# A two-layer graph network on one core: the ReLU of an attention head moved from ScalarE to one VectorE product, a residual input made later, and a half-speed TensorE in the planner that writes the order

## Chip, cores and metric

The kernel runs on one core of one Trainium2 chip. The metric is device time in microseconds (us) of one execution; the profile adds, for one execution, what every engine did and when. In what follows PE is TensorE (its matmuls; PEld its weight loads), DVE is VectorE, ACT is ScalarE, POOL is GpSimd and SP is SyncE.

## The reference

Sixteen graphs of 1024 nodes with 256 features go through two layers, all in float32. Cut to what matters:

```python
# layer 0: graph attention with 4 heads of 64 features, one edge type present
h = einsum('bnd,hde->bhne', x, W)
weight = leaky_relu(e_src[:, None] + e_dst[None, :]);  weight[adj == 0] = -1e9
dst = softmax(weight) @ h + bias
out = relu(dst) + h                       # per head
out = (out - mean) / sqrt(var + 1e-6) * gamma + beta       # per head
x = layernorm(x + out)
# layer 1: self-attention with 8 heads of 32 features, query = key = value, then an MLP
n = layernorm(x);  a = softmax(where(adj > 0, n n^T / sqrt(32), -inf)) @ n
x1 = x + a;  y = layernorm(x1)
x = layernorm(x + x1 + gelu(y @ W1 + b1) @ W2 + b2)
```

## The kernel before

**Tiling.** A graph is cut into 8 blocks of 128 rows and 2 halves of 512 queries. There is no loop on the chip: Python writes out all instructions of the 16 graphs, one list for each engine, and the engines run their lists in that order (the four compute engines are scheduled by hand).

**Two streams.** `layer0()` and `layer1()` are Python generators, and the writer takes steps from one or the other, so that layer 0 of graph b+1 is interleaved with layer 1 of graph b. Layer 0 of a graph is `prepare` (transposes of `xk` and of the adjacency block `ak`, products with `w0e`, into `acc` banks of PSUM) and `attention0` (for each half and head two groups of 64 matmuls `acc<-v,p`, whose weights `p` are products on DVE). Layer 1 is `attention1` (64 steps in two halves, two groups of heads and eight key blocks: four matmuls `ps<-nT`, four exponentials on ACT, two mask products on DVE, then `po<-p,v`, `po<-p,unit`, `po<-v,p`) and `mlp` (`ps<-yT,w_sb`, GELU on ACT into `hid`, `po<-w_sb,hid`).

**Chains.** What follows a head or a half is a generator too, called a chain. `residual0` is the one the change rewrites: when a head of layer 0 is complete in its `acc` bank, with the sums of the weights in a 65th column, it takes the reciprocal of the sums (`ranges<-acc` on DVE), lets ACT write `relu<-acc,ranges` in four pieces of 128x64, and adds the result to `hb` on DVE. `after0` then normalises a pair of heads, and after the last pair makes the whole row's norm: `sq<-hb,t,r` on ACT (the tile `normed`), its transposes `acc<-ident,sq`, the scaled copies `nT`, the transposes back `acc<-ident,nT`, the copies `v` (the tile `v1`), and at its end `x1`, four ACT products of 128x256, which layer 1 needs as its residual input only after its attention. A chain says with `yield engine, needs...` on what it waits; `advance()` runs it when the planner's clock says that these are there. `finish_norms(b, n)` runs a half's chain to its end at once, if layer 1 asks for the half before that.

**Banks.** `bank0` hands out two PSUM banks (`acc0`, `acc1`) in turn. A bank is free when the chain that reads it has been written down; on the chip the first matmul into it waits for the last read.

**The planner.** The class `Pace` wraps every engine. `enter` keeps for each engine the time when it becomes free, for each tile when it is written and read, and adds `cost` for each instruction. These times decide nothing on the chip, they decide the order only: which stream goes next, and when a chain is advanced. `COURSE` says how far layer 0 is to be for each amount of layer 1 done: a list of (work of layer 1, graphs of layer 0), linear between. Because every instruction passes through `Engine.call`, nearly all rows of the profile carry line 61; rows are told apart by their tiles. Names in the profile leave out trailing digits, so `v0` and `v1` both read `v`, `x1` reads `x`, and `p0` reads `p`.

Of the kernel before, what the change touches and what calls it, by code (L numbers as in the profile page):

```python
# [35 lines left out]
AF = mybir.ActivationFunctionType  # L36
OP = mybir.AluOpType
PSUM = bass.MemoryType.PSUM

P = 128  # L40
# [9 lines left out]
class Engine:  # L50


    def __init__(self, pace, name):
        self.pace, self.name = pace, name
# [35 lines left out]
class Pace:  # L90
# [5 lines left out]
    def __init__(self, nc):  # L96
        self.nc = nc
        self.free = dict.fromkeys(self.LATENCY, 0.0)
        self.written, self.read = {}, {}
        self.array = self.table = self.last = None  # L100

        self.born = self.settle = lambda tile: None
        for name in self.LATENCY:
            setattr(self, name, Engine(self, name))
# [38 lines left out]
    def enter(self, engine, op, args, kwargs):  # L143
        aps = [a for a in (*args, *kwargs.values()) if isinstance(a, bass.AP)]
        out, ins = aps[0].tensor.name, [a.tensor.name for a in aps[1:]]
        if op == "dma_start":
            start = max(self.now(), self.through(out))
            self.written[out] = start + self.LATENCY["sync"]
            return
        start = max(  # L150
            [self.free[engine], self.read.get(out, 0.0)] + [self.written.get(i, 0.0) for i in ins if i != out]
        )
        end = self.free[engine] = start + self.cost(engine, op, aps, args[2] if len(args) > 2 else None)
        self.written[out] = max(self.written.get(out, 0.0), end + self.LATENCY[engine])
        if "accum_out" in kwargs:
            out = kwargs["accum_out"].tensor.name
            self.written[out] = max(self.written.get(out, 0.0), end + self.LATENCY[engine])
        for i in ins:
            self.read[i] = max(self.read.get(i, 0.0), end)
# [3 lines left out]
def fast_path(  # L163
# [24 lines left out]
    nc = Pace(tc.nc)  # L188
    B, N, D = x.shape
    H0, _, HO = w0.shape  # L190
# [9 lines left out]
    BPH = HALF // P  # L200
# [66 lines left out]
    for i, (src, queue, _) in enumerate(terms):  # L267
        for pair in range(H0 // PAIR):
# [3 lines left out]
                    tensor=src.tensor,  # L272
# [11 lines left out]
    for i, (_, _, dst) in enumerate(terms):  # L284
        for c in range(DC):
            t = two.tile([P, H0, HO], F32, name="z")
# [17 lines left out]
    def at_time(t):  # L304
        return lambda: t
# [28 lines left out]
    def power(src, n, name):  # L334
        r = small.tile([P, n], F32, name=name)
        nc.gpsimd.tensor_tensor(r, src, mhalf[:, :n], op=OP.pow)
        return r

    def statistics(src, mv):
        st = small.tile([P, 6], F32, name="st", passing=True)  # L340
        nc.vector.bn_stats(st, src)
        nc.vector.bn_aggr(mv, st)

    def minus_mean(mean, r, n):
        t = small.tile([P, n], F32, name=f"t{n}")
        nc.vector.scalar_tensor_tensor(t, mean, -1.0, r, op0=OP.mult, op1=OP.mult)
        return t
# [97 lines left out]
    def complete(chain):  # L445

        for item in list(chains):
            if item[0] is chain:
                while item in chains:
                    run(item)  # L450


    def load_x(t, b, k, count):
        nc.sync.dma_start(t, x[b, k * P : (k + count) * P, :].rearrange("(g p) d -> p g d", p=P))
# [161 lines left out]
    def residual0(av, h, rinv):  # L616

        t = two.tile([P, BPH, HO], F32, name="relu")
        nc.vector.reciprocal(rinv, av[:, :, HO])
        yield "scalar", rinv  # L620
        for q in range(BPH):
            nc.scalar.activation(t[:, q, :], av[:, q, 0:HO], AF.Relu, scale=rinv[:, q : q + 1])
        yield "vector", t
        nc.vector.tensor_add(h, h, t)

    def after0(b, n, hd, o):


        for first in range(hd + 1):
            complete(residuals[b, n, first])  # L630
        rowwise = [P, BPH, D]
        heads = slice((hd - PAIR + 1) * HO, (hd + 1) * HO)
        oh = o[:, :, heads].rearrange("p g (h e) -> p g h e", e=HO)
        per_head = [P, BPH, PAIR, HO]
        s = small.tile([P, BPH, PAIR], F32, name="s0")
        nc.vector.tensor_reduce(s, oh, axis=mybir.AxisListType.X, op=OP.add)
        nc.vector.scalar_tensor_tensor(
            oh, s[:, :, :, None].to_broadcast(per_head), -1.0 / HO, oh, op0=OP.mult, op1=OP.add
        )
        yield "scalar", o  # L640
        sq = two.tile([P, BPH, PAIR * HO], F32, name="oT1")
        nc.scalar.activation(sq, o[:, :, heads], AF.Square)
        if hd == H0 - 1:
            xl = one.tile(rowwise, F32, name="xl")
            load_x(xl, b, n * BPH, BPH)
        yield "vector", sq
        v = small.tile([P, BPH, PAIR], F32, name="v0s")
        nc.vector.tensor_reduce(
            v, sq.rearrange("p g (h e) -> p g h e", e=HO), axis=mybir.AxisListType.X, op=OP.add
        )  # L650
        nc.vector.tensor_scalar(v, v, 1.0 / HO, EPS_HEAD, op0=OP.mult, op1=OP.add)
        r = power(v.rearrange("p g e -> p (g e)"), BPH * PAIR, "r0").rearrange("p (g e) -> p g e", e=PAIR)
        pair = o[:, :, heads]
        nc.vector.tensor_mul(pair, pair, lng0_r[:, None, heads].to_broadcast([P, BPH, PAIR * HO]))
        if hd == H0 - 1:
            nc.vector.tensor_add(xl, xl, lnb0_r[:, None, :].to_broadcast(rowwise))
        yield "vector", r
        nc.vector.tensor_mul(oh, oh, r[:, :, :, None].to_broadcast(per_head))
        if hd < H0 - 1:
            return  # L660
        complete(norms[b, n, PAIR - 1])
        nc.vector.tensor_add(o, o, xl)
        yield "vector", o
        mv = small.tile([P, BPH, 2], F32, name="mv0")
        for g in range(BPH):
            statistics(o[:, g, :], mv[:, g, :])

        v2 = small.tile([P, 2, BPH], F32, name="v2")  # L670
        nc.vector.tensor_scalar(v2[:, 0, :], mv[:, :, 1], 1.0 + EPS, EPS * EPS, op0=OP.mult, op1=OP.add)
        r2 = power(v2[:, 0, :], BPH, "r2")
        nc.vector.tensor_scalar(v2[:, 1, :], mv[:, :, 1], EPS, None, op0=OP.add)
        r3 = power(v2[:, 1, :], BPH, "r3")
        yield "vector", r2
        t = minus_mean(mv[:, :, 0], r2, BPH)
        yield "scalar", t
        normed = one.tile(rowwise, F32, name="sq")
        scale_shift(normed, o, t, r2, BPH)
        yield "tensor", normed, side_ready  # L680
        nT = two.tile([P, DC, HALF], F32, name="nT")
        for g in range(0, BPH, GB):
            transpose_rows(nT[:, :, g * P : (g + GB) * P], normed[:, g : g + GB, :], g1_c, be1_c)
            yield "tensor", normed, side_ready
        yield "tensor", nT, side_ready
        v1 = two.tile([P, BPH, H1, HD + 1], F32, name="v1")
        nc.vector.memset(v1[:, :, :, HD], 1.0)
        for g in range(0, BPH, GB):
            pt = side_bank([P, GB, DC, P])
            for i in range(GB):  # L690
                for c in range(DC):
                    nc.tensor.transpose(pt[:, i, c, :], nT[:, c, (g + i) * P : (g + i + 1) * P], ident)
            nc.scalar.copy(
                v1[:, g : g + GB, :, 0:HD], pt.rearrange("p g c (h e) -> p g (c h) e", e=HD)
            )
            yield "tensor", nT, side_ready
        handed[b, n] = [None, v1, nT]
        yield "vector", r3

        ratio = small.tile([P, BPH], F32, name="ratio")  # L700
        nc.vector.tensor_mul(ratio, v2[:, 0, :], r2)
        nc.vector.tensor_mul(ratio, ratio, r3)
        yield "scalar", ratio
        x1 = three.tile(rowwise, F32, name="x1")
        for g in range(BPH):
            nc.scalar.mul(x1[:, g, :], normed[:, g, :], ratio[:, g : g + 1])
        handed[b, n][0] = x1
# [271 lines left out]
    ATTN1 = 2.0 + 2.5 * (NH * NB * H1 // QUAD)  # L979
    WORK1 = ATTN1 + NB // GB * (1.75 * FC / 2 + 3.5 * GB)  # L980
    SLACK = 0.06
    COURSE = [(0.0, 1.0), (ATTN1, 1.40), (WORK1 - 10.0, 2.0), (WORK1, 2.0)]

    def wanted():
        b, done = place[1]
        for (start, low), (end, high) in zip(COURSE, COURSE[1:]):
            if done < end:
                return b + low + (high - low) * (done - start) / (end - start)
        return b + COURSE[-1][1]

# [470 lines left out]
```

## Time and profile before

| what | value |
| --- | --- |
| median of 3 runs | 3663.35 us (3662.82 to 3672.89) |
| the profiled execution: its own time, its span | 3667.81 us, 3665.6 us |
| mean granted TensorE clock | 0.976 |
| busy share: PE, PEld, DVE, ACT, POOL | 96%, 65%, 77%, 60%, 12% |
| instructions | 142190 |
| `relu<-acc,ranges` on ACT, 128x64 | 512 times, 319 ns each, 118.2 us |
| `hb<-hb,relu` on DVE, 128x256 | 128 times, 424 ns each, 54.2 us |
| `x<-sq,ratio` on ACT (the tile x1), 128x256 | 128 times, 501 ns each, 54.6 us |

A row of groups names line, engine, operation, output and inputs, shapes and count, then the busy time, the mean of one instruction, and the idle time of that engine just before, with what ended it. A row of the timeline gives start, length, engine, output and inputs and a count, and in square brackets the idle time before it. A float32 matmul appears as two records. The row of a window gives the busy time of each engine, and behind POOL the granted TensorE clock, where 1.00 is full speed, the share of the DMA engines and the GB/s moved.

### The profile page before, as it was taken

Reading aid. Unit: us, or ns where it says so; the run is one execution under the profiler, and the core shown is the slowest. Engines: PE = TensorE matmul, PEld = TensorE weight load, DVE = VectorE, ACT = ScalarE, POOL = GpSimd, SP = SyncE. Lnnn points to the kernel's source line nnn. Section 1 sums busy time; section 2 is a strip of 40 time slices with the busy share of each in tenths; the row PEclk is TensorE's granted clock in tenths of the full one; section 3 lists DMA queues with packets and bytes.
Section 4 is the critical chain, followed back from the end, with each engine's and each line's share of the span. In section 5 each row is a group of like instructions: output and inputs, shape, how many; then the busy total and the mean of one; then the engine's idle time right before and its main releaser. Section 6 shows DMA issues by size and latency. Waiting matters only on the chain.

```text
span 3665.6 us, 142190 instructions
## 1 busy us (share of the span) xinstructions
PE 3506.3 (96%) x64673; PEld 2368.4 (65%) x64673; DVE 2840.2 (77%) x4882; ACT 2191.5 (60%) x5024; POOL 428.7 (12%) x424
## 2 busy tenths in 40 slices
PE   6899999999999999999999999999999999999998
PEld 4567575675856658576585766757567585665846
DVE  5787787878878787787887868778787887878784
ACT  2665746557475574746647466574755747557474
POOL 0102011010110101101020110201101011010100
PEclk9899999999999999999999999999999999999999
DMA  4111101011010110201101011110101102010000
GB/s 102 33 18 33 29 14 37 15 37 24 15 41 11 36 23 16 45 6 40 20 27 34 13 35 17 33 29 14 39 14 35 26 14 43 11 36 9 16 6 14
DMA packets 77525, 97.30 MB, mean 27 GB/s; under 512 B 9072, under 2 KB 59760, under 8 KB 76912
## 3 DMA queue, kind: packets, MB, share of 16 engines
q0 software_dynamic: 18432, 33.56, 6.1%
q1 hardware_dynamic: 56896, 53.50, 4.6%
q8 instruction: 508, 8.32, 0.9%
q10 hardware_dynamic: 1584, 1.05, 0.1%
q14 instruction: 105, 0.86, 0.1%
HBM read 104.87 MB, written 16.78 MB: 33 GB/s over the span
## 4 chain that ended last, share of the span: by engine, by line
PE 87%; ACT 8%; DVE 3%; issue 1%; DMA 0%; ACTq 0%; POOL 0%; POOLq 0%; DVEq 0%
PE ps L61 33%; PE po L61 33%; PE acc L61 21%; ACT p L61 3%; DVE p L61 2%; ACT mask L61 1%; ACT sq L61 1%; ACT nT L61 1%; ACT v L61 0%; ACT relu L61 0%; DMA w0e<-in_L_gnn_W_dram 0%; ACT z L61 0%; ACT cb L61 0%; DVE z L61 0%; ACT oT L61 0%
## 5 line engine op out<-in xcount | busy, mean ns | idle before, releaser
L61 ACT ACTIVATE p<-ps 128x512 f32<-128x512 f32 x2048 | 1061.8, 617 | 402.1 <-PE ps L61 402.1
L61 DVE TENSOR_TENSOR p<-p,mask 128x1024 f32<-128x1024 f32 x1024 | 1187.9, 1218 | 103.0 <-ACT p L61 101.3
L61 PE MATMUL ps<-nT 32*128 32x512 f32 x4096 | 795.4, 654 | 11.0 <-ACT cb L61 9.8
L61 DVE SCALAR_TENSOR_TENSOR p<-cb,dinv,mask 128x512 f32<-128x512 f32 x1024 | 698.9, 744 | 28.6 <-ACT cb L61 28.6
L61 PEld LDWEIGHTS po<-v,p 128*32 128x32 f32 x32768 | 401.1, 111 | 323.5 <-issue 279.7
L61 PE MATMUL acc<-v,p 128*64 128x65 f32 x16384 | 546.2, 225 | 28.6 <-ACT relu L61 13.2
L61 PEld LDWEIGHTS acc<-v,p 128*64 128x64 f32 x16384 | 507.4, 139 | 96.1 <-issue 47.4
L61 PE MATMUL po<-p,v 128*32 128x512 f32 x2048 | 559.1, 621 | 0.0
L61 PE MATMUL po<-p,unit 128*32 128x512 f32 x2048 | 558.5, 621 | 0.0
L61 ACT ACTIVATE hid<-ps,b_sb 128x256 f32<-128x256 f32 x512 | 241.4, 476 | 437.1 <-PE ps L61 435.0
L61 PE MATMUL ps<-yT,w_sb 128*128 128x256 f32 x2048 | 480.0, 384 | 0.0
L61 PE MATMUL po<-w_sb,hid 128*128 128x256 f32 x2048 | 477.0, 384 | 0.0
L61 PEld LDWEIGHTS po<-w_sb,hid 128*128 128x128 f32 x2048 | 382.4, 190 | 74.5 <-issue 22.7
L61 PEld LDWEIGHTS ps<-yT,w_sb 128*128 128x128 f32 x2048 | 379.8, 190 | 51.8
L61 PE MATMUL po<-v,p 128*32 128x33 f32 x32768 | 392.5, 199 | 4.6 <-issue 4.5
L61 PEld LDWEIGHTS ps<-nT 32*128 32x128 f32 x4096 | 284.9, 187 | 153.2 <-ACT p L61 52.0
L61 PEld LDWEIGHTS po<-p,v 128*32 128x32 f32 x2048 | 79.4, 109 | 339.9 <-DVE p L61 171.9
L61 POOL TENSOR_TENSOR r<-v,mhalf 128x1 f32<-128x1 f32 (+1 forms) x192 | 168.0, 880 | 574.7 <-DVE v L61 540.1
L61 DVE TENSOR_TENSOR z<-acc,bias_r 128x256 f32<-128x256 f32 x128 | 54.2, 423 | 219.5 <-ACT hb L61 217.8
L61 POOL TENSOR_TENSOR r<-v1s,mhalf 128x4 f32<-128x4 f32 x32 | 61.9, 1934 | 1214.9 <-DVE v1s L61 1214.9
L61 POOL TENSOR_TENSOR r<-v0s,mhalf 128x8 f32<-128x8 f32 x64 | 128.9, 2014 | 522.6 <-DVE v0s L61 522.6
L61 POOL DMA_DIRECT2D ak<-in_adj_dram x128 | 69.8, 545 | 914.3 <-PE acc L61 903.9
(113 smaller groups left out, 3078.8 us busy)
## 6 DMA issues: line engine op xcount, KB each, us to landing
ak<-in_adj_dram POOLq DMA_DIRECT2D x128, 256.0 KB, 4.0
xk<-in_x_dram SPq DMA_DIRECT2D x64, 256.0 KB, 3.4
xl<-in_x_dram SPq DMA_DIRECT2D x32, 512.0 KB, 4.0
out_dram<-z SPq DMA_DIRECT2D x128, 128.0 KB, 1.7
w_sb<-in_L_gnn_W_dram SPq DMA_DIRECT2D x2, 1024.0 KB, 6.6
v<-in_L_gnn_a_src_dram SPq DMA_DIRECT2D x2, 320.0 KB, 4.9
v<-in_L_gnn_a_dst_dram ACTq DMA_DIRECT2D x1, 320.0 KB, 7.0
xl<-in_L_gnn_a_dst_dram ACTq DMA_DIRECT2D x1, 320.0 KB, 6.2
```

Of the source, the lines that this page charges most:

```text
L61: return method(*args, **kwargs)
```

## The change

Four edits. `residual0` no longer goes to ACT: after the reciprocal one DVE instruction takes the maximum with zero and multiplies with the reciprocal, spread over the 64 columns of each piece, and the add to `hb` follows without a `yield`. `after0` asks for a time 12 us later on the planner's clock before it writes `x1`. `Pace.enter` doubles the cost of a TensorE instruction that starts within 3 us after TensorE waited for more than 1.5 us. `COURSE` has 1.42 in place of 1.40 at the end of layer 1's attention.

```diff
@@ class Pace, __init__
+        self.slow = 0.0
@@ class Pace, enter
-        end = self.free[engine] = start + self.cost(engine, op, aps, args[2] if len(args) > 2 else None)
+        cost = self.cost(engine, op, aps, args[2] if len(args) > 2 else None)
+        if engine == "tensor":
+            if start > self.free[engine] + 1.5:
+                self.slow = start + 3.0
+            if start < self.slow:
+                cost *= 2.0
+        end = self.free[engine] = start + cost
@@ residual0
         nc.vector.reciprocal(rinv, av[:, :, HO])
-        yield "scalar", rinv
-        for q in range(BPH):
-            nc.scalar.activation(t[:, q, :], av[:, q, 0:HO], AF.Relu, scale=rinv[:, q : q + 1])
-        yield "vector", t
+        nc.vector.scalar_tensor_tensor(
+            t, av[:, :, 0:HO], 0.0, rinv[:, :, None].to_broadcast([P, BPH, HO]), op0=OP.max, op1=OP.mult
+        )
         nc.vector.tensor_add(h, h, t)
+        yield from ()
@@ after0
-        yield "scalar", ratio
+        yield "scalar", ratio, at_time(nc.now() + 12.0)
         x1 = three.tile(rowwise, F32, name="x1")
@@ fast_path
-    COURSE = [(0.0, 1.0), (ATTN1, 1.40), (WORK1 - 10.0, 2.0), (WORK1, 2.0)]
+    COURSE = [(0.0, 1.0), (ATTN1, 1.42), (WORK1 - 10.0, 2.0), (WORK1, 2.0)]
```

## The prediction

> **What bounds the kernel now.** I read the page's busy line first, then the waits of PE, then stretches of 5 us with their clock, then the timeline where they are bad.
>
> ```profile
> PE 3506.3 (96%) x64673; PEld 2368.4 (65%) x64673; DVE 2840.2 (77%) x4882; ACT 2191.5 (60%) x5024; POOL 428.7 (12%) x424
> ...
> PE 87%; ACT 8%; DVE 3%; issue 1%; DMA 0%; ACTq 0%; POOL 0%; POOLq 0%; DVEq 0%
> ```
>
> PE is busy for 96% and holds 87% of the chain that ended last. Two things can be had: PE's idle time, 3665.6 - 3506.3 = 159 us, and the time at lowered clock, 3665.6 x (1 - 0.976) = 88 us. The waits of PE (total, times, longest) say for whom it is idle:
>
> ```profile
> PE acc L61 <- ACT mask L61: 37.3, 34, 9.7
> PE acc L61 <- ACT nT L61: 18.7, 19, 1.1
> PE acc L61 <- ACT relu L61: 14.5, 17, 1.4
> PE acc L61 <- DVE z L61: 13.1, 37, 1.8
> ...
> PE acc L61 <- ACT v L61: 10.7, 15, 0.7
> ```
>
> The counts of 15 to 19 and 34 say one or two places per graph. A graph takes 223 us (the `sq` at 1700.3 returns at 1923.6), and its worst place is where layer 1 of a graph begins:
>
> ```profile
> 1700.00:1705.00 5.00, 3.84 (x14) 2.08 (x13) 3.23 (x5) 5.00 (x12) 0.00 (x0) 0.63 0.72 128
> 1705.00:1710.00 5.00, 5.00 (x80) 2.18 (x76) 4.06 (x8) 3.65 (x11) 0.00 (x0) 0.50 0.00 0
> 1710.00:1715.00 5.00, 3.16 (x38) 2.29 (x26) 1.58 (x2) 2.98 (x7) 0.00 (x0) 0.85 0.01 3
> ```
>
> Here ACT is full in the first row, PE idles in the first and third, and the clock is 0.63, 0.50 and 0.85. The timeline names the waits (brackets), and a second place later in the graph:
>
> ```profile
> 1700.83 1.72 PE L61 MATMUL acc<-w0e,xT 128*128 128x264 f32 x4 [0.28 <-DVE z L61]
> ...
> 1703.43 1.11 PE L61 MATMUL acc<-ident,sq 128*128 128x128 f32 x4 [0.88 <-ACT mask L61]
> ...
> 1712.35 1.09 PE L61 MATMUL acc<-ident,nT 128*128 128x128 f32 x8 [1.11 <-ACT nT L61]
> ...
> 1714.17 0.66 PE L61 MATMUL acc<-ident,xk 128*128 128x128 f32 x4 [0.73 <-ACT v L61]
> ...
> 1813.38 0.95 ACT L61 ACTIVATE relu<-acc,ranges 128x64 f32<-128x64 f32 x4
> 1814.36 0.42 DVE L61 TENSOR_TENSOR hb<-hb,relu 128x256 f32<-128x256 f32 x1 [1.67 <-ACT relu L61]
> 1814.38 2.08 PE L61 MATMUL acc<-v,p 128*64 128x65 f32 x64 [0.79 <-ACT relu L61]
> ```
>
> The boundary costs 0.28 + 0.88 + 1.11 + 0.73 = 3.0 us of idle per graph, and the clock. The relu costs 0.79 us: the bank is free only when ACT has read it, and ACT came to it after four exponentials.
>
> [...] with the run cut into 4 us slices the 14 boundaries from 356 to 3268 us lose (slice times one minus clock, summed) close to 1.7, 3.4, 5.1 or 6.8 us, half of one to four such windows; 63 us in all, 4.5 each. [...] 128x256 takes 425 ns in `o<-acc,ranges` from PSUM and 424 in `hb<-hb,relu` from SBUF. [...]
>
> **Part 1, the relu.** Gone from ACT: 512 x 319 ns = 118.2 us. New on DVE: 128 products of 128x256 with a spread operand out of PSUM; no row shows this form, the nearest is `o<-acc,ranges` (425 ns, spread operand, PSUM)[...]; I take 0.43, 128 x 0.43 = 55 us (bounds 54 to 64). DVE also loses a wait: before `hb<-hb,relu` it stood idle for 156.4 us in 94 cases, mask products queued behind. So DVE ends about 100 us freer, though busier on paper (79%). The bank is now released in DVE's own queue, ahead of the weights `p` for the next group that would use the bank, so PE cannot wait for the relu longer than for its own weights. The 14.5 us go. What is late next there is DVE's mask product: at 1824.18 PE waits 0.41 in the middle of `po<-v,p` (4.5 us in 9 such cases). DVE is full from 1814 to 1826 and now gets 1.67 - 0.43 = 1.2 us back; but the changed order leaves no `acc` group between the last steps of layer 1's attention as a filler, so I book 2 of the 4.5. In the first 110 us layer 0 runs alone and DVE is the bound there: eight products add 3.4 us, the waits for relu that vanish give 2.36 + 0.20 + 0.43; nil. **Sum: -16.5 us.**
>
> **Part 2, the order.** I compared the compiled lists of both kernels. The same matmuls run, changes between matmul shapes are 2098 against 2099, and SP and POOL have equally many rows (DMA issues and powers), so nothing is added. From graph 1 to 13 all graphs have one pattern, so one boundary counts for 15. In it the second transpose of `sq` goes ahead of the first `po` group, a full step (`ps<-nT`, then `po`) lies between the transposes of `nT` and those of `xk`, and ACT writes `sq` ahead of `z` and the small copies. By the durations of the trace: exponentials end at 1699.38; `sq` takes 1.96, to 1701.34; `z` and copies 0.94, to 1702.28; DVE's `z` 0.42 more, so the second `w0e` product begins at 1702.77 in place of 1700.83: **1.94 us more wait**. `mask` ends at 1703.38 as before, so the 0.88 go, and `sq` is transposed at 1704.5, 1.06 later. Then `ps` and the second `sq` to 1709.3; `nT` on ACT to 1710.7; the `po` group covers it until 1712.05 at half clock: 1.11 gone. The `v` copies end near 1713.8, and a step of 2.7 us covers them: 0.73 gone. Per graph 1.94 - 0.88 - 1.11 - 0.73 = -0.78; 15 times, **-11.8 us**. Bounds: +1.06 if the later waits come back elsewhere, -2.7 if `z` is on time.
>
> The clock: from 1704.5 PE now has no gap until the `xk` transposes[...]. That ends the cases of four windows (five of 14) a window or more earlier; against it stands a single gap of 2.2 us. I take half a window less on average, 0.5 x 1.7 x 15 = **-12.8 us** (bounds: one window more, +25; two less, -50).
>
> The steps moved take their DMAs along: the second `ak` turn of the boundary comes one step (3 us) later, and with it POOL's load of the block three ahead; POOL idles 18.8 us before that issue and the load lands in 4.0, so nothing waits.
>
> **Part 3, x1 later.** 128 x 501 ns stay on ACT. For a graph's second half nothing moves: layer 1 asks for it, the chain is forced to its end, and `x1` follows the copies `v` directly in both lists. It delays the next exponentials by 1.7 us, against which PE has a `po` group (1.6). In the first half it lies in the MLP stage, where PE shows 5.00 of 5.00 from 1830 to 1910: nil.
>
> **Total:** -16.5 - 11.8 - 12.8 = -41 us. The profiled execution took 3667.8, so about 3627 for one like it; it stands 4.5 above the median 3663.35, so 3622 against the median.
>
> **Rivals.**
> - *The single gap halves the clock for longer (slower).* [...] With one window more, 1.7, and +1.06 of gaps: 15 x 2.77 = +41.5, less 16.5: +25, **3688**. It decides once the clock costs more than 1.1 us more per graph with the later gaps back. For it: one to four windows happen now[...]. Against: PE is gapless afterwards.
> - *Nothing but the relu.* Boundary gains and losses cancel, or new waits on DVE (55 us more work) eat them: -5 to -16, **3653**. For it: ACT is full at the boundary before and after.
> - *The half clock nearly goes.* If `z` arrives early and one window remains, clock 4.5 - 1.7 = 2.8 and idle 2.0 less per graph: 15 x 4.8 + 16.5 = -88, **3575**.
> - *The planner's edits do nothing*: excluded, since the lists differ.
>
> **How the numbers follow.** Forecast 0.60, slower rival 0.13, relu only 0.12, clock gone 0.15. A difference of 0.3% (11 us) is about what a measurement can tell from none. Faster: 0.60 + 0.15 and a part of relu only = 0.77; same 0.10; slower 0.13. The range takes in most of the third rival and stops short of the slower one: 3565 to 3662.
>
> **What would show it.** Right: no wait of PE for relu; PE's waits for `nT` and `v` near zero; one wait for `z` of about 2 us per graph; the mean clock at 0.979 or more; ACT busy near 2073, DVE near 2895; `relu` on DVE at 0.43 us. Wrong: a clock under 0.976, a `z` wait well under 1 us, or new waits of PE for DVE's `p`.

## The result, and the profile after

The changed kernel takes 3603.46 us (median of 4 runs, 3601.67 to 3610.08) against 3663.09 us (4 runs): 59.6 us less, ratio 0.9835 with the 95% interval 0.9813 to 0.9856. The forecast was 3622, range 3565 to 3662: right in sign and in range, and a third short in size (41 of 60). The profiled execution has a span of 3608.3 us, 57.3 below that of before, at a mean clock of 0.981.

The page's busy line and the engines' shares of the chain, after:

```profile
PE 3478.7 (96%) x64673; PEld 2365.7 (66%) x64673; DVE 2901.0 (80%) x5010; ACT 2088.0 (58%) x4512; POOL 419.1 (12%) x424
...
PE 91%; ACT 6%; DVE 2%; issue 1%; DMA 0%; ACTq 0%; POOL 0%; POOLq 0%; DVEq 0%
```

PE still bounds the kernel. Its idle time fell from 159.3 to 129.6 us, its busy time by 27.6 us for the same matmuls. The waits of PE (total, times, longest):

```profile
PE acc L61 <- DVE z L61: 41.4, 22, 6.0
PE acc L61 <- ACT mask L61: 18.8, 19, 10.3
...
PE acc L61 <- ACT nT L61: 3.2, 7, 1.1
...
PE acc L61 <- DVE relu L61: 2.0, 1, 2.0
...
PE acc L61 <- ACT v L61: 0.7, 1, 0.7
```

The 14.5 us for ACT's relu are gone (one wait of 2.0 for DVE's, at 114 us, is left), `nT` fell by 15.5, `v` by 10.0, `mask` by 18.5, and `z` rose by 28.3. The same boundary as before, in 5 us stretches, with the one wait of PE that the timeline shows between 1676 and 1692 us, and the new product by its tile (minimum, median, maximum in ns; first and last start in us):

```profile
1675.00:1680.00 5.00, 2.78 (x10) 1.46 (x9) 2.22 (x4) 5.00 (x14) 0.58 (x2) 0.79 0.70 131
1680.00:1685.00 5.00, 5.00 (x23) 2.59 (x21) 4.61 (x6) 4.00 (x12) 0.00 (x0) 0.53 0.00 0
1685.00:1690.00 5.00, 4.97 (x122) 2.54 (x123) 2.92 (x6) 4.84 (x11) 0.00 (x0) 1.00 0.01 3
```

```profile
1679.21 2.13 PE L61 MATMUL acc<-w0e,xT 128*128 128x264 f32 x4 [2.22 <-DVE z L61]
```

```profile
L61 DVE SCALAR_TENSOR_TENSOR relu<-acc,ranges x128: 423/425/426, 62.1 to 3414.6; 128x256 f32<-128x256 f32 x128
```

The wait is the one that the prediction worked out, 0.28 + 1.94 = 2.22 us. After it the timeline shows no further wait of PE, and the clock is full again in the third stretch. From the `sq` of graph 1 (356.04 us before, 357.99 after) to that of graph 14 (3266.02 and 3212.77) a graph takes 223.84 and 219.60 us, so these 13 graphs hold 55.2 of the 57.3 us.

To see the clock I cut the stretch from 12 us ahead of each boundary's `sq` to 24 us behind it into slices of 1 us; twice the sum of one minus clock is the time at half clock. A window, below, is 3.41 us at half clock: in the traces of before and changed the stretches at 0.50 between 300 and 3400 us last 3.41 us, or two (before: up to four) times that. Means over the 13 boundaries of graphs 2 to 14, of one profiled execution each; the rows from relu_swap on are the experiments told below:

| kernel | ratio to before, 95% | half clock per boundary, us | PE idle there, us |
| --- | --- | --- | --- |
| before | 1 | 8.9 | 3.4 |
| changed | 0.9835 (0.9813 to 0.9856) | 4.7 | 2.3 |
| relu_swap | 0.9944 (0.9926 to 0.9961) | 8.9 | 3.5 |
| plan_only | 0.9912 (0.9894 to 0.9930) | 5.8 | 1.7 |
| relu_only | 1.0022 (1.0013 to 1.0031) | 4.5 | 3.8 |
| no_slow | 0.9987 (0.9978 to 0.9996) | 5.3 | 3.8 |
| no_course | 0.9842 (0.9827 to 0.9857) | 4.5 | 2.3 |
| sq_late | 0.9885 (0.9866 to 0.9904) | 5.3 | 1.7 |
| warm | 0.9793 (0.9779 to 0.9806) | 0.0 | 0.7 |
| warm2 | 0.9799 (0.9782 to 0.9815) | 0.0 | 1.5 |
| warm_sq | 0.9795 (0.9782 to 0.9808) | 1.3 | 1.0 |
| warm_before | 0.9906 (0.9890 to 0.9923) | 2.6 | 2.6 |

### The profile page after: what moved, and what is told of

Read it like the earlier page. It is cut to its first block, busy times and chain, and to the rows that moved or that the text cites. A ratio compares the mean times of both kernels' runs of the same rounds, so it can differ in the third digit from the quotient of the medians.

```text
span 3608.3 us, 141736 instructions
## 1 busy us (share of the span) xinstructions
PE 3478.7 (96%) x64673; PEld 2365.7 (66%) x64673; DVE 2901.0 (80%) x5010; ACT 2088.0 (58%) x4512; POOL 419.1 (12%) x424
## 4 chain that ended last, share of the span: by engine, by line
PE 91%; ACT 6%; DVE 2%; issue 1%; DMA 0%; ACTq 0%; POOL 0%; POOLq 0%; DVEq 0%
PE po L61 35%; PE ps L61 34%; PE acc L61 22%; ACT p L61 2%; ACT mask L61 1%; DVE p L61 1%; ACT sq L61 1%; ACT xT L61 0%; ACT z L61 0%; ACT nT L61 0%; ACT cb L61 0%; DVE z L61 0%; DVE hb L61 0%; DMA w0e<-in_L_gnn_W_dram 0%; DMA v<-in_L_gnn_a_dst_dram 0%
## 5 line engine op out<-in xcount | busy, mean ns | idle before, releaser
L61 PE MATMUL acc<-v,p 128*64 128x65 f32 x16384 | 550.5, 226 | 20.1 <-DVE p L61 14.5
L61 PE MATMUL po<-p,v 128*32 128x512 f32 x2048 | 547.5, 610 | 0.0
L61 PE MATMUL po<-p,unit 128*32 128x512 f32 x2048 | 547.1, 609 | 0.0
L61 POOL TENSOR_TENSOR r<-v,mhalf 128x1 f32<-128x1 f32 (+1 forms) x192 | 158.3, 830 | 724.5 <-DVE v L61 396.8
L61 PE MATMUL acc<-w0e,xT 128*128 128x264 f32 x512 | 156.4, 430 | 46.7 <-DVE z L61 33.2
```

The source lines that it names most:

```text
L61: return method(*args, **kwargs)
```

## The experiments

My theory: the relu edit is worth the waits that it removes, and the rest is the new order at the boundary, in gaps and in clock. The rival: the freed engines pay, in any order. Any edit makes the planner write another order, so the two must be held apart by force.

**relu_swap: the old order, the new product.** The planner goes on booking four ScalarE instructions, and the product is put in their place.

```diff
         yield "scalar", rinv
         for q in range(BPH):
-            nc.scalar.activation(t[:, q, :], av[:, q, 0:HO], AF.Relu, scale=rinv[:, q : q + 1])
+            nc.enter("scalar", "activation", (t[:, q, :], av[:, q, 0:HO], AF.Relu), {"scale": rinv[:, q : q + 1]})
+        nc.nc.vector.scalar_tensor_tensor(
+            t, av[:, :, 0:HO], 0.0, rinv[:, :, None].to_broadcast([P, BPH, HO]), op0=OP.max, op1=OP.mult
+        )
         yield "vector", t
```

> The order of the kernel before, kept as it was (the planner still books the four ScalarE instructions), with the one VectorE product in their place. My account (the relu edit is worth its own waits, the rest comes from the order): PE's wait for relu, 14.5 us, goes, the waits for nT, v and mask at the boundary of a graph stay within 3 us of 18.7, 10.7 and 37.3; -10 to -22 us, ratio to before 0.994 to 0.997. Rival (freeing 118 us of ScalarE and 100 us of VectorE is what pays, in any order): -45 us or more, ratio under 0.988, with less clock loss too.

Measured: 0.9944, some 20 us. The waits of PE:

```profile
PE acc L61 <- ACT mask L61: 29.1, 33, 1.4
PE acc L61 <- ACT nT L61: 18.7, 19, 1.1
...
PE acc L61 <- ACT v L61: 10.5, 15, 0.7
```

`nT` and `v` stand where they stood, no wait for relu is left, and the half clock is unchanged at 8.9 us. (`mask` lost only its longest wait, 9.7 us at the start, which this profile books under "issue".) Apart from the relu's own rows, the rows of DVE, ACT, POOL and SyncE in this trace are those of before, in the same sequence. The edit by itself is worth about its own waits, 14.5 us against an interval of 14 to 27: my account.

**plan_only: the new planner, the old ReLU.** The changed kernel with `residual0` as before.

> The planner's edits of the change (half clock behind waits, 1.42, the later x1) with the ReLU left on ScalarE in four pieces; the TensorE list is close to that of the changed kernel. My account: the waits for nT and v near zero, a wait for z of about 2 us per graph, the wait for relu still there at 14 us or so; -30 to -45 us, ratio 0.988 to 0.992, and with relu_swap it adds up to the whole -60. Rival (the order needs the freed engines): under 15 us gained, ratio over 0.996.

Measured: 0.9912, some 33 us. From its waits of PE:

```profile
PE acc L61 <- ACT relu L61: 16.8, 17, 4.6
...
PE acc L61 <- DVE z L61: 8.7, 23, 0.7
...
PE acc L61 <- ACT nT L61: 3.0, 7, 1.1
```

My account again, with one miss: `z` is 8.7 us in all, not 2 per graph. In this order `sq` still stands behind the small copies; the 2.2 us wait needs both edits. The two parts make 53 of 60 us; by the intervals the rest is not told apart from nothing.

**relu_only: the relu edit with the old planner.** The kernel before with `residual0` as in the changed kernel.

> The relu edit alone, the order planned anew by the old planner with 1.40. My account: the gain of relu_swap plus or minus what the new boundary order happens to give; -5 to -35 us, ratio 0.990 to 0.999. Rival (relu is the change): -50 to -60 us, ratio 0.984 to 0.986.

Measured: 1.0022, slower by some 8 us: outside both expectations. The waits of PE, with the same product in an order that the old prices wrote:

```profile
PE acc L61 <- ACT oT L61: 47.2, 31, 2.6
PE acc L61 <- DVE z L61: 42.0, 37, 3.1
PE acc L61 <- ACT nT L61: 25.1, 32, 1.6
```

The edit that is worth 20 us in place lost them, and more, to the order it caused.

**no_slow and no_course: which planner edit it is.** The changed kernel without the doubled cost, and with 1.40 for 1.42.

```diff
# no_slow
-            if start < self.slow:
-                cost *= 2.0
# no_course
-    COURSE = [(0.0, 1.0), (ATTN1, 1.42), (WORK1 - 10.0, 2.0), (WORK1, 2.0)]
+    COURSE = [(0.0, 1.0), (ATTN1, 1.40), (WORK1 - 10.0, 2.0), (WORK1, 2.0)]
```

> The changed kernel with the planner's old pricing of TensorE (no half clock behind waits), 1.42 and the ReLU on VectorE. relu_only, with the old pricing and 1.40, was at 1.0022 with PE waits of 47 us for oT, 42 for z and 25 for nT. If the half-clock pricing is what orders the boundary well: 0.997 to 1.003 here, with waits for oT and nT near those of relu_only. If the 1.42 is: 0.982 to 0.986, as the changed kernel.

> The changed kernel with 1.40 in place of 1.42, the half-clock pricing kept. If the pricing orders the boundary well: 0.982 to 0.987, as the changed kernel. If the 1.42 is: 0.995 to 1.003. If both are needed, each of the two kernels without one lies at 0.990 or above.

Measured: 0.9987 and 0.9842. The half-clock price makes the order; 1.42 is not told apart from 1.40 by these intervals. The waits of no_slow, and one from its timeline:

```profile
PE acc L61 <- ACT oT L61: 40.6, 16, 2.6
PE acc L61 <- DVE z L61: 38.5, 22, 3.0
PE acc L61 <- ACT nT L61: 23.5, 31, 1.1
```

```profile
1744.21 1.12 PE L61 MATMUL acc<-ident,oT 128*128 128x128 f32 x4 [2.61 <-ACT oT L61]
```

Once per graph PE stands 2.61 us before the transposes of the first heads' output, and these then take 1.12 us, where the same four took 0.66 in the kernel before. Four transposes of that shape (`sq`, at 1703.43) took 1.11 us there with the clock at 0.50: by its times, a second place at half clock. The mean clock of the span, 0.974 in no_slow and 0.978 in relu_only against 0.981 in the changed kernel, with 5.3, 4.5 and 4.7 us at the boundary, says too that in these two the table, which sees the boundary alone, shows a part of the half clock only.

The fourth edit, `x1` later, changes nothing: the lists of all five engines of the changed kernel come out the same with it and without it.

**sq_late: is the 2.2 us wait dear?** The changed order with ScalarE's `sq` moved behind `z` and the small copies, by holding the four instructions back until the copy to `hb` is written.

> The changed kernel with one thing moved: at the boundary of a graph ScalarE writes the four pieces of sq behind z and the small copies of the w0e product instead of ahead of them (as in the kernel before); all else in the same order. My account (the 2.2 us wait for z comes from that place): the wait for z falls by about 1.9 us per graph, a wait for mask of 0.9 us per graph comes back, sq is transposed 1 us earlier, and the long gap no longer lowers the clock: 15 to 30 us below the changed kernel, ratio to before 0.976 to 0.980. Rival (ScalarE is the bound from the first exponentials to the copies v and does the same work in either order): within 4 us of the changed kernel, ratio 0.983 to 0.985.

Measured: 0.9885, some 19 us worse than the changed kernel. Both expectations missed. The wait for `z` did go (41.4 to 14.2 us), PE idles less at the boundary (1.7 us for 2.3), and the half clock is about as long (5.3 for 4.7). Its place differs. Counted from the end of the exponentials ahead of `sq`, it begins at 1.9 to 4.7 us in the changed kernel, where PE waits for `z` until 3.4; in sq_late it begins at 3.4 to 6.7 us at eight of the ten boundaries that have any, where PE's last wait, for `mask`, ends at about 4.1. A graph that starts with two such windows takes about 221 us here and 220 there; with none, 218.2 to 218.8 in both. So the gap itself costs little: ACT does the same work in either order. What costs is the clock, and by its place: in the changed kernel two windows that begin at 1.9 to 2.4 us go with graphs of 219.0 to 219.9 us, two that begin at 4.5 to 4.7 with 220.6 to 221.2.

**warm, warm_sq, warm2: the gap filled.** Idle TensorE products go where PE waits, into a `po` bank that nobody reads: four ahead of the second `w0e` product (warm), two there (warm2), or in sq_late two ahead of the transposes of `sq` (warm_sq).

```diff
+                if b >= 2 and k == 0 and g == 1:
+                    ...
+                    for f in range(4):
+                        idle = ps_o.pool.tile([P, D], F32, name="po")
+                        nc.nc.tensor.matmul(idle, ident, w2_sb[:, f, :], start=True, stop=True)
                 ph, _ = bank0([P, D + 2 * H0])
```

> The changed kernel with four idle TensorE products of 128x256 (weights w2_sb against the identity, into a po bank that nobody reads) ahead of the second w0e product, at 14 of the 15 boundaries: they fill about 1.9 of the 2.2 us that PE waits for z. If that gap is what halves the clock: the slices of lowered clock at the boundary go from a mean of 4.8 us to under 2, and the time falls by 10 to 20 us below the changed kernel, ratio to before 0.978 to 0.981. If the clock falls for the thin load of the whole stretch (transposes, products of 32 rows), nothing changes: within 4 us of it, 0.983 to 0.985.

> The kernel sq_late with two such idle products between the second w0e product and the transposes of sq, where it waits 0.9 us for mask. sq_late lost 19 us to the changed kernel although PE waits less in it; its half clock begins 1 to 4 us later, in the products behind the wait. If that lateness is the cause, filling the gap brings the clock back and the time to 0.978 to 0.983; if its order costs for another reason, it stays at 0.987 to 0.990.

> The kernel warm with two idle products in place of four: the wait of 2.2 us shrinks to about 1.3. warm lost all half clock at the boundaries and was at 0.979, the changed kernel with the full gap has 4.7 us of it and 0.9835. If a gap of 1.3 us is short enough: no half clock, 0.978 to 0.981. If it is not: 3 to 5 us of half clock remain and the ratio is 0.982 to 0.985.

Measured: 0.9793, 0.9795 and 0.9799, the fastest kernels of this study; warm is at 3592.31 us. The timeline and the stretches of warm, from the same `sq` on:

```profile
1665.53 1.99 PE L523 MATMUL po<-w_sb,ident 128*128 128x256 f32 x8
1667.83 1.16 PE L61 MATMUL acc<-w0e,xT 128*128 128x264 f32 x4 [0.30 <-DVE z L61]
```

```profile
1664.24:1669.24 5.00, 4.70 (x21) 2.95 (x19) 2.23 (x4) 5.00 (x15) 0.00 (x0) 1.00 0.69 134
1669.24:1674.24 5.00, 5.00 (x90) 2.73 (x88) 4.51 (x9) 5.00 (x15) 0.00 (x0) 1.00 0.00 0
1674.24:1679.24 5.00, 4.62 (x96) 2.79 (x96) 3.10 (x4) 4.73 (x11) 0.00 (x0) 1.00 0.01 3
```

The idle products take 1.99 us of the wait, and the clock stays at 1.00: no half clock at any of the 14 boundaries that were filled. sq_late's loss is gone as well with its fill. There nine of the 14 filled boundaries have full clock; at five one window of half clock remains, from 1.8 to 2.0 us after the exponentials' end, where PE otherwise waits for `mask`. The graphs that begin so take no longer than the rest (218.4 to 218.9 us against 218.1 to 218.9, the last graph left out): what the half clock costs depends on where it falls. Two products do as well as four.

**warm_before: the fill without the change.** Two idle products in the kernel before, ahead of the transposes of `sq`.

> The kernel before with two idle TensorE products of 128x256 between the second w0e product and the transposes of sq, where PE waits 0.9 us for mask, at 14 boundaries; ReLU and order as before. In the kernel before a mean of 8.9 us at the boundary runs at half clock, and a graph with one window (3.4 us) takes about 222.3 us against 223.8 on average. If the first gaps of the boundary start the half clock: it goes to under 3 us, and 25 to 40 us are gained, ratio 0.989 to 0.993, without any edit of the change. If the later waits for nT (1.1 us) and v (0.7 us) do, which stay: under 12 us gained, ratio over 0.996, half clock over 5 us.

Measured: 0.9906 (3633.37 us). The order and the relu are as before, and so are these waits:

```profile
PE acc L61 <- ACT nT L61: 18.7, 19, 1.1
PE acc L61 <- ACT relu L61: 14.5, 17, 1.3
...
PE acc L61 <- ACT v L61: 10.9, 15, 0.7
```

Yet 33 us come back, and the half clock falls from 8.9 to 2.6 us. So most of it started in the stretch of the first gaps, not at the later ones. Whether the shorter gap or the added work did it, this run does not say; see "What holds the clock" below.

## Why the prediction was right, and where it fell short

- **Part 1, relu, -16.5:** right. In place it measured some 20 (interval 14 to 27). The product takes 425 ns (0.43 taken), DVE grew by 61 us (55). One product in the text is wrong without harm: 512 x 319 ns is 163 us; 118.2 is the time during which at least one piece ran, as they overlap. They overlap their neighbours too, so ACT fell by 103.5 only. DVE's 156.4 us of waits for ACT's relu are gone.
- **Part 2, gaps, -11.8:** right by name, and nearly in size. `z` +28.3 (29.1 expected), `nT` and `v` -25.5 (27.6), but `mask` -18.5 (13.2). The 0.88 us for `mask` was read at a boundary whose `w0e` product ran mostly at half clock (1.72 us); at 12 of 14 boundaries that product takes 1.16 us and the wait is 1.43 to 1.44, as in the row below. Not foreseen: the waits for `oT`, from 10.6 to 4.0 us, against 3.0 new ones for `xT`.

```profile
1926.73 1.11 PE L61 MATMUL acc<-ident,sq 128*128 128x128 f32 x4 [1.43 <-ACT mask L61]
```

- **Part 2, clock, -12.8:** the term that was mis-sized. The text gave half a window less per graph, 0.85 us. The slices show 8.9 - 4.7 = 4.2 us less at half clock, 1.2 windows, worth at most half of it, 2.1 us per graph or 31 us in all. The mean clock of the whole span gives 3665.6 x 0.024 - 3608.3 x 0.019 = 19 us, because ahead of 300 us and behind 3400 us the changed kernel loses some 9 us more than before. PE's busy time, for the same matmuls, fell by 27.6 us, and its idle time by 29.7, where parts 1 and 2 had 28.3: nearly all that the forecast lacks is clock.
- **The reason given for the clock** is shown in part. Of the boundaries of graphs 2 to 14, five before had four windows and none after has more than two, as foretold. But the text laid the long cases to the later gaps, for `nT` and `v`, and warm_before kept both and lost 6.3 of 8.9 us. That the gaps make the half clock was my estimate and is not shown: 3.41 us in which PE was busy for 92% were followed by half clock (below).
- **Part 3, x1, nil:** right, and for a stronger reason: the edit moves nothing.
- **Rivals.** That the single gap of 2.2 us would lengthen the half clock is refuted: with it the half clock fell from 8.9 to 4.7 us, and sq_late, without that gap, has no less (5.3) and was slower. "Nothing but the relu" fell to plan_only. The half clock that nearly goes is what warm reached, at 3592 where I had put 3575.
- What I did not see is how far the relu edit depends on the planner: alone, in the order that the old planner wrote for it, it loses. From plan_only to the changed kernel it is worth some 28 us, which the intervals do not tell apart from the 20 in the old order.

**What holds the clock.** The fill both shortens the wait and adds dense products, and no run separates the two. Two stretches of 3.41 us of the kernel before, each with the one behind it, show that PE's busy share alone does not tell where the half clock comes:

```profile
1697.88:1701.29 3.41, 3.13 (x14) 1.64 (x12) 3.13 (x5) 3.41 (x12) 1.81 (x3) 1.00 0.40 49
1701.29:1704.70 3.41, 2.53 (x10) 1.36 (x10) 2.22 (x2) 3.41 (x9) 0.00 (x0) 0.50 0.70 143
1711.54:1714.95 3.41, 1.87 (x14) 1.49 (x14) 0.04 (x1) 2.66 (x7) 0.00 (x0) 1.00 0.00 0
1714.95:1718.36 3.41, 3.41 (x92) 1.89 (x94) 0.89 (x1) 3.41 (x9) 0.00 (x0) 1.00 0.23 77
```

In the first PE is busy for 92%, and the clock behind it is 0.50. In the third it is busy for 55%, with transposes alone, and the clock behind it is 1.00. So of these two it is the one with less idle time that half clock follows. They also differ in the size of their products. An estimate from the rows of the trace: rows x columns of the weights as a share of 128*128, for 0.84 ns per moved column (a 128x256 float32 record starts every 216 ns in dense stretches; half of that in bf16, where a 128x128 record starts every 56 ns against 109), makes about 1.25 us of full-size product in the first and 1.47 us in the third. Two stretches alone do not show that the clock goes with it.

**Open.** No run set the work of such a stretch by itself. Nor do the runs price every place of the half clock, so how much of sq_late's 19 us is place is not shown; that filling removes the loss is shown.

## What to carry to other kernels

When an edit changes what a planner sees, measure it in the old order too: here one product was worth 20 us in place and cost 8 in the order that it caused. Where TensorE waits a microsecond or two in the midst of thin work, look at the granted clock behind the wait before shortening the wait: two idle matmuls at each boundary won 33 us, and moving the wait away lost 19. Price the half clock in the model that writes the order.

## What was not expected of the hardware

- Half clock came with short gaps: in the kernel before 0.28 us and then 0.64 to 1.44 us, with a mean of 8.9 us at half clock per boundary. Two products ahead of the second gap (four took 1.99 us in warm) took 6.3 of these away.
- A wait of 2.2 us left 0 to 6.8 us of half clock from one graph to the next, with the same instructions. With two idle products in that wait (warm2) it was 0 at every filled boundary.
